# Layer-norm statistics from rows instead of from partition blocks, in an attention kernel that is bound by TensorE

## The chip, the cores and the metric

One core of one Trainium2 chip. The metric is the device time of one execution in microseconds (us).

## The reference

128 graphs of 128 nodes with 768 features. Cut to what matters:

```python
h = jnp.maximum(_layernorm(x, axis=-1), 0.0)          # mean and variance over 768, eps 1e-5
q, k, v = (split_heads(h @ W + b) for W, b in ...)    # 12 heads of 64
scores = q @ k.T / sqrt(64) + beta * adj              # -9e15 where adj == 0
out = x + softmax(scores) @ v
```

All is float32.

## The kernel before

The 128 graphs go in 32 groups of 4. In each group TensorE computes three "slices" of projections, called qk0, v and qk1, with a scheme of 15 block products a slice in place of 18. The scores and the weighted sums of the attention stand between these products. While TensorE works on group G, the other engines prepare group G + 1. `then(n, f)` hangs work behind product n of a slice; the scheduler may place it earlier in an engine's queue, unless `tc.issue_after(ins)` queues it behind the instruction `ins` of the same engine (order alone, no wait).

x is loaded in blocks: partition block a of 32 holds features 192a to 192a + 191, so that VectorE's transpose of 32 x 32 squares later gives the layout TensorE needs. A row's 768 features then lie in four partition blocks, and its statistics must be summed over partitions. Two small matmuls do that:

```python
def stats(G, g):                       # VectorE: 16 of these a group
    ...
    for b in range(NB):
        nc.vector.bn_stats(st[G][:, g * NB + b, :], xg[G, g][:, b, :])

def moments_1(G, lo, hi):
    bank = pm[G, lo, "bank"] = take()
    ...
    for q in range(0, P, HD):          # sums over the four blocks
        nc.tensor.matmul(pm[G, lo][q:q + HD, 0], mean8...[:, q:q + HD], halves(G, lo, hi, 1), start=True, stop=True)
    nc.vector.tensor_reduce(mean, ...)
    ...                                # three more small VectorE instructions
def moments_2(G, lo, hi, mean, d):
    for q in range(0, P, HD):
        nc.tensor.matmul(pm[G, lo][q:q + HD, 1], mean8...[:, q:q + HD], d, start=True, stop=True)
    ...
    nc.gpsimd.tensor_tensor(r, ve, nhalf.to_broadcast([P, n]), ALU.pow)      # 128 x 16
    shifted = nc.gpsimd.tensor_tensor(t, mean, r, ALU.mult)

def norm(G, g):                        # ScalarE: 16 a group
    for b in range(NB):
        ...
        nc.scalar.activation(t, t, AF.Relu, bias=shift[G, n], scale=rstd[G, n])
```

The adjacency of the next group passes through VectorE, and its square through ScalarE:

```python
def bias_1(G, raw):
    nc.vector.transpose(a, raw...)                                   # adjT
    nc.vector.tensor_scalar(kp, a, 0.0, None, op0=ALU.is_gt)
    nc.vector.tensor_scalar(a, a, beta_c, ..., op0=ALU.mult, op1=ALU.min)
    ...                                                              # GpSimd fills t
    nc.vector.copy_predicated(t, kp, a)                              # biasT
    if G:
        nc.scalar.activation(a, a, AF.Square, scale=...)             # square
def bias_2(G, a):
    nc.vector.tensor_reduce(bm, a, AX.X, ALU.max)                    # the maximum, reads the square
    nc.vector.tensor_tensor(seen[:, 16:20], seen[:, 16:20], bm, ALU.max)
```

The partial sums of the products lie in PSUM banks, 8 in all. After its product, VectorE adds a bank to its result (L352, L361) or ScalarE copies it (L357). TensorE may write a bank again only after that.

## Time and profile before

| | before |
|---|---|
| time, median of 6 runs | 2892.97 us (2892.39 to 2894.02) |
| span of the profiled run | 2891.4 us |
| busy: TensorE, VectorE, ScalarE, GpSimd | 100%, 68%, 28%, 13% |
| one steady group | 89.40 us |

The prediction below shows the lines of this profile. The way to read it: TensorE is busy in every window from its beginning to its end, at full clock. What does not take TensorE's time, and does not let it wait, costs nothing.

### The profile page before, as it was taken

The numbers are of one execution on the slowest core, as the hardware profiler recorded it, in microseconds if no ns is written. First come the engines' busy times: TensorE is split into PE (matmuls) and PEld (weight loads), VectorE is DVE, ScalarE is ACT, GpSimd is POOL, SyncE is SP. The second block draws the span as 40 slices with busy tenths as digits, with TensorE's granted clock in tenths as the row PEclk, the third lists the DMA queues.
The fourth block names the chain that finished last, engine by engine and source line by source line (L and its number), as shares of the span: only waits on it lengthen the run. The fifth ranks groups of instructions, "written<-read, shape, count | busy, mean of one in ns | idle before, by whom it ended". The sixth has DMA issues, their size and how long they took to land.

```text
span 2891.4 us, 81358 instructions
## 1 busy us (share of the span) xinstructions
PE 2879.8 (100%) x35562; PEld 2020.5 (70%) x35562; DVE 1961.4 (68%) x4743; ACT 801.3 (28%) x1750; POOL 370.9 (13%) x304
## 2 busy tenths in 40 slices
PE   9999999999999999999999999999999999999999
PEld 7666677666777676777667766677666677666766
DVE  7866667666676666767667676667666676666665
ACT  2432322222222323223232232322223222322221
POOL 1111111111111111111111111111111111111110
PEclk9999999999999999999999999999999999999999
DMA  6322122221222111221112212122221222111211
GB/s 166 78 56 57 39 62 71 60 56 44 54 71 63 52 51 47 71 68 52 56 42 67 71 50 61 40 63 71 56 60 39 58 71 60 56 48 47 67 41 39
DMA packets 357784, 172.16 MB, mean 60 GB/s; under 512 B 84400, under 2 KB 357040, under 8 KB 357424
## 3 DMA queue, kind: packets, MB, share of 16 engines
q1 hardware_dynamic: 355552, 166.53, 21.3%
q8 instruction: 279, 4.57, 0.7%
q10 hardware_dynamic: 1872, 0.40, 0.1%
q14 instruction: 81, 0.66, 0.1%
HBM read 116.53 MB, written 50.33 MB: 58 GB/s over the span
## 4 chain that ended last, share of the span: by engine, by line
PE 96%; issue 2%; DVE 1%; DMA 0%; POOL 0%; ACT 0%; SPq 0%; ACTq 0%; POOLq 0%; DVEq 0%
PE bank L336 82%; PE bank L382 6%; PE bank L417 6%; PE bank L498 1%; DMA x<-in_x_dram 0%; POOL rstd L262 0%; DVE S L286 0%; ACT x L273 0%; DVE qk L361 0%; POOL xo L422 0%; PE bank L241 0%; DVE A L280 0%; PE bank L255 0%; PE bank L437 0%; PE bank L549 0%
## 5 line engine op out<-in xcount | busy, mean ns | idle before, releaser
L336 PE MATMUL bank<-S,qk_T 128*64 128x256 f32 x7056 | 822.6, 380 | 1.1 <-ACT qk L357 0.8
L336 PEld LDWEIGHTS bank<-S,qk_T 128*64 128x64 f32 x7056 | 503.4, 137 | 257.6 <-issue 4.1
L361 DVE TENSOR_TENSOR qk<-qk,bank 128x512 f32<-128x512 f32 x630 | 428.6, 681 | 340.1 <-PE bank L336 338.1
L357 ACT ACTIVATE qk<-bank,bqk 128x256 f32<-128x256 f32 x756 | 311.5, 471 | 1010.6 <-PE bank L336 812.6
L336 PE MATMUL bank<-A,qk_T 128*64 128x256 f32 x4032 | 478.6, 379 | 0.9 <-DVE qk L361 0.9
L336 PE MATMUL bank<-S,qk_B 128*64 128x256 f32 x4032 | 478.2, 379 | 1.0 <-DVE qk L361 1.0
L422 POOL TENSOR_TENSOR xo<-xo,o 128x512 f32<-128x512 f32 x189 | 252.2, 1334 | 1601.4 <-DVE o L401 1343.3
L336 PE MATMUL bank<-v_T,S 128*64 128x256 f32 x3584 | 422.6, 380 | 0.0
L352 DVE TENSOR_TENSOR v<-v,bank 128x512 f32<-128x512 f32 x320 | 220.0, 687 | 296.1 <-PE bank L336 296.1
L389 ACT ACTIVATE e<-e 128x512 f32<-128x512 f32 x378 | 227.2, 630 | 661.0 <-DVE e L386 660.5
L336 PEld LDWEIGHTS bank<-A,qk_T 128*64 128x64 f32 x4032 | 284.3, 137 | 137.5 <-DVE qk L361 1.1
L336 PEld LDWEIGHTS bank<-S,qk_B 128*64 128x64 f32 x4032 | 278.6, 137 | 128.9 <-DVE qk L361 1.5
L336 PEld LDWEIGHTS bank<-v_T,S 128*64 128x64 f32 x3584 | 252.3, 137 | 126.3 <-issue 5.7
L273 ACT ACTIVATE x<-x,shift,rstd 128x192 f32<-128x192 f32 x504 | 224.3, 533 | 350.1 <-POOL shift L264 350.1
L336 PE MATMUL bank<-v_B,S 128*64 128x256 f32 x2048 | 244.1, 380 | 0.0
L386 DVE SCALAR_TENSOR_TENSOR e<-bank,biasT 128x512 f32<-128x512 f32 x378 | 231.2, 680 | 16.7 <-PE bank L382 16.7
L336 PE MATMUL bank<-v_T,A 128*64 128x256 f32 x2048 | 237.9, 379 | 0.0
L417 PEld LDWEIGHTS bank<-v,e 128*64 128x64 f32 x6048 | 208.6, 138 | 27.3
L280 DVE STREAM_TRANSPOSE A<-x 128x256 f32<-128x256 f32 x378 | 212.0, 613 | 4.0 <-ACT x L273 4.0
L417 PE MATMUL bank<-v,e 128*64 128x65 f32 x6048 | 208.3, 221 | 0.0
L347 DVE TENSOR_TENSOR v<-bv_b,bank 128x512 f32<-128x512 f32 x192 | 131.8, 686 | 112.0 <-PE bank L336 112.0
L230 DVE BATCH_NORM_STATS2 st<-x 128x6 f32<-128x192 f32 x504 | 154.3, 344 | 76.5 <-DMA x<-in_x_dram 76.4
(83 smaller groups left out, 1688.3 us busy)
## 6 DMA issues: line engine op xcount, KB each, us to landing
x<-in_x_dram SPq DMA_DIRECT2D x504, 96.0 KB, 2.6
xo<-in_x_dram SPq DMA_DIRECT2D x189, 256.0 KB, 2.9
out_dram<-xo SPq DMA_DIRECT2D x189, 256.0 KB, 2.5
adj<-in_adj_dram SPq DMA_DIRECT2D x128, 64.0 KB, 2.4
qk_T<-in_L_gnn_Wq_dram SPq DMA_DIRECT2D x10, 128.0 KB, 4.1
qk_T<-in_L_gnn_Wk_dram SPq DMA_DIRECT2D x10, 128.0 KB, 4.0
v_T<-in_L_gnn_Wv_dram SPq DMA_DIRECT2D x5, 256.0 KB, 6.0
qk_B<-in_L_gnn_Wq_dram SPq DMA_DIRECT2D x8, 128.0 KB, 3.9
```

The lines of the kernel that those rows point to most:

```text
L230: nc.vector.bn_stats(st[G][:, g * NB + b, :], xg[G, g][:, b, :])
L273: nc.scalar.activation(t, t, AF.Relu, bias=shift[G, n], scale=rstd[G, n])
L280: last = nc.vector.transpose(t[:, :, g * N:(g + 1) * N].rearrange("p c (b i) -> p c b i", i=SQ), src)
L336: nc.tensor.matmul(p[q:q + HD, i, :], lhs[:, q:q + HD], rhs, start=(first and i == 0 and c == 0), stop=(c == 1), skip_group_check=True)
L352: added[G] = nc.vector.tensor_tensor(o, o, got, ALU.add if sign > 0 else ALU.subtract)
L357: nc.scalar.activation(t[:, i, :], p[:, i, :], AF.Identity, bias=bqk[:, i, oc:oc + 1], scale=float(sign))
L361: added[G] = nc.vector.tensor_tensor(t, t, p, ALU.add if sign > 0 else ALU.subtract)
L382: nc.tensor.matmul(ps[oc, i][k:k + HD, g * N:(g + 1) * N], t[r, 1, at][:, k:k + HD], t[r, 0, at], start=True, stop=True)
L386: taken[0] = nc.vector.scalar_tensor_tensor(e, ps[oc, i].rearrange("p (g n) -> p g n", g=GRP), SCORE_CAP * ISCALE, biasT[G], op0=ALU.min, ...
L389: nc.scalar.activation(e, e, AF.Exp, scale=1.0 / ISCALE)
L417: nc.tensor.matmul(pa[q:q + HD, 2 * g + i, :], es[G, oc, i][:, 2 * r + g, q:q + HD], vt[G, "v", r, h // 4][:, 4 * g + h % 4, :], start=Tru ...
L422: nc.gpsimd.tensor_add(t, t, o.rearrange("p a (b j) d -> p (a b) (j d)", j=2))
```

## The change

Its intent is to take the two sums over partitions off TensorE. x is loaded a second time, by rows, so that VectorE can compute a row's statistics alone. The results are then a column per row and must be spread to the four partition blocks; 16 transfers of 1 KB from SBUF to SBUF do that. SBUF is full, so the half rows use the two adjacency buffers. The adjacency is therefore loaded after them (and ahead of the small transfers), and its VectorE work is queued in v instead of floating into qk0. Cut to its core:

```diff
+    def load_halves(G, g):
+        for h in range(2):
+            t = rows[G, g, h] = work.tile([P, VH], F32, tag=("adj", "adjT")[h], ..., bufs=1)
+            nc.sync.dma_start(t, x[G * GRP + g, :, h * VH:(h + 1) * VH])
+    def row_stats(G, g):
+        ...
+        for h in range(2):
+            nc.vector.bn_stats(rows[G][:, g, h, :], rows[G, g, h])
+        nc.vector.bn_aggr(rows[G, "mv"][:, g, :], rows[G][:, g])
+    def row_moments(G):
+        ...
+        nc.gpsimd.tensor_tensor(t[:, 0], ve, nhalf.to_broadcast([P, GRP]), ALU.pow)      # 128 x 4
+        nc.gpsimd.tensor_tensor(t[:, 1], mean, t[:, 0], ALU.mult)
+        for b in range(NB):
+            for a in range(NB):
+                nc.sync.dma_start(to[a * SQ:(a + 1) * SQ, b], t[b * SQ:(b + 1) * SQ])
+        def behind(f, *args):
+            with tc.issue_after(added[G].ins):      # added: the latest add of a product
+                return f(*args)
 ... in qk0 of group G
-                    then(11 + g, lambda g=g: stats(G + 1, g))
+                    then((0, 5, 8, 11)[g], lambda g=g: load_halves(G + 1, g))
+                    then((4, 7, 10, 13)[g], lambda g=g: behind(row_stats, G + 1, g))
+            if G > 1:
+                then(14, lambda: raw.append(load_adj(G + 1)))
+                then(14, lambda: row_moments(G + 1))
 ... in v of group G
-                then(at + 5 + g, lambda g=g: norm(G + 1, g))
+                then(at + 5 + g, lambda g=g: behind(norm, G + 1, g) if G > 1 else norm(G + 1, g))
-            then(at, lambda: got.extend(moments_1(G + 1, 0, GRP * NB)))
-            then(at + (3 if G else 2), lambda: moments_2(G + 1, 0, GRP * NB, *got[:2]))
+            if G < 2:
+                ... (the two lines above)
-                then(8, lambda: got.append(bias_1(G + 1, load_adj(G + 1))))
+                then(8, lambda: got.append(behind(bias_1, G + 1, raw.pop()) if raw else bias_1(G + 1, load_adj(G + 1))))
```

The `behind` around the normalization orders nothing: `added` is an instruction of VectorE, the normalization runs on ScalarE, and `issue_after` orders within one engine only.

More of the change, by code (lines that the diff above doesn't have):

```diff
@@ L267, in moments_2 @@
         return shifted
+    rows = {}
+    def load_halves(G, g):
+        for h in range(2):
+            t = rows[G, g, h] = work.tile([P, VH], F32, tag=("adj", "adjT")[h], name=f"half_{G}_{g}_{h}", bufs=1)
+            nc.sync.dma_start(t, x[G * GRP + g, :, h * VH:(h + 1) * VH])
+    def row_stats(G, g):
+        if g == 0:
+            rows[G] = stat.tile([P, GRP, 2, nc.vector.BN_STATS_DIM], F32, tag="strow", name=f"strow_{G}", bufs=1)
+            rows[G, "mv"] = stat.tile([P, GRP, nc.vector.BN_AGGR_DIM], F32, tag="mvrow", name=f"mvrow_{G}", bufs=1)
+        for h in range(2):
+            nc.vector.bn_stats(rows[G][:, g, h, :], rows[G, g, h])
+        nc.vector.bn_aggr(rows[G, "mv"][:, g, :], rows[G][:, g])
+    def row_moments(G):
+        mv = rows[G, "mv"]
+        ve = stat.tile([P, GRP], F32, tag="verow", name=f"verow_{G}", bufs=1)
+        nc.vector.tensor_scalar(ve, mv[:, :, 1], EPS, None, op0=ALU.add)
+        mean = stat.tile([P, GRP], F32, tag="meanrow", name=f"meanrow_{G}", bufs=1)
+        nc.vector.tensor_scalar(mean, mv[:, :, 0], -1.0, None, op0=ALU.mult)
+        t = stat.tile([P, 2, GRP], F32, tag="row2", name=f"row2_{G}", bufs=1)
+        nc.gpsimd.tensor_tensor(t[:, 0], ve, nhalf.to_broadcast([P, GRP]), ALU.pow)
+        nc.gpsimd.tensor_tensor(t[:, 1], mean, t[:, 0], ALU.mult)
+        to = stat.tile([P, NB, 2, GRP], F32, tag="block2", name=f"block2_{G}", bufs=1)
+        for b in range(NB):
+            for a in range(NB):
+                nc.sync.dma_start(to[a * SQ:(a + 1) * SQ, b], t[b * SQ:(b + 1) * SQ])
+        for g in range(GRP):
+            for b in range(NB):
+                rstd[G, g * NB + b], shift[G, g * NB + b] = to[:, b, 0, g:g + 1], to[:, b, 1, g:g + 1]
     def norm(G, g):
@@ L524, in rows_1 @@
         t = xg[0, g].rearrange("p b f -> p (b f)")
-        s = stat.tile([P, 2, nc.vector.BN_STATS_DIM], F32, tag="strow", name=f"strow_{g}", bufs=2)
+        s = stat.tile([P, 2, nc.vector.BN_STATS_DIM], F32, tag="strow_0", name=f"strow0_{g}", bufs=2)
         for h in range(2):
@@ L530, in rows_1 @@
                 nc.vector.bn_stats(s[:, h, :], t[:, h * VH:(h + 1) * VH])
-        mv = stat.tile([P, nc.vector.BN_AGGR_DIM], F32, tag="mvrow", name=f"mvrow_{g}", bufs=2)
+        mv = stat.tile([P, nc.vector.BN_AGGR_DIM], F32, tag="mvrow_0", name=f"mvrow0_{g}", bufs=2)
         nc.vector.bn_aggr(mv, s)
-        ve = stat.tile([P, 1], F32, tag="verow", name=f"verow_{g}", bufs=2)
+        ve = stat.tile([P, 1], F32, tag="verow_0", name=f"verow0_{g}", bufs=2)
         first["ve"] = nc.vector.tensor_scalar(ve, mv[:, 1:2], EPS, None, op0=ALU.add)
@@ L609, in behind_scores @@
             return f(*args)
-    early = []
+    early, raw = [], []
     for G in range(NG):
@@ L626, in direct @@
                 elif G:
-                    then(11 + g, lambda g=g: stats(G + 1, g))
+                    then((0, 5, 8, 11)[g], lambda g=g: load_halves(G + 1, g))
+                    then((4, 7, 10, 13)[g], lambda g=g: behind(row_stats, G + 1, g))
+            if G > 1:
+                raw = []
+                then(14, lambda: raw.append(load_adj(G + 1)))
+                then(14, lambda: row_moments(G + 1))
         if not G:
@@ L650, in direct @@
                     then(g, lambda g=g: stats(G + 1, g))
-                then(at + 5 + g, lambda g=g: norm(G + 1, g))
-            then(at, lambda: got.extend(moments_1(G + 1, 0, GRP * NB)))
-            then(at + (3 if G else 2), lambda: moments_2(G + 1, 0, GRP * NB, *got[:2]))
+                then(at + 5 + g, lambda g=g: behind(norm, G + 1, g) if G > 1 else norm(G + 1, g))
+            if G < 2:
+                then(at, lambda: got.extend(moments_1(G + 1, 0, GRP * NB)))
+                then(at + (3 if G else 2), lambda: moments_2(G + 1, 0, GRP * NB, *got[:2]))
             if G:
-                then(8, lambda: got.append(bias_1(G + 1, load_adj(G + 1))))
-                then(12, lambda: bias_2(G + 1, got[2]))
+                then(8, lambda: got.append(behind(bias_1, G + 1, raw.pop()) if raw else bias_1(G + 1, load_adj(G + 1))))
+                then(12, lambda: bias_2(G + 1, got[-1]))
             else:
```

## The prediction

> **What bounds the kernel now.** I read first the page's busy shares and its chain of what ended last, then the windows of one steady group of four graphs (31.6 us of first projection slice "qk0", 29.1 of "v", 28.7 of "qk1"), then the timelines of TensorE, VectorE, ScalarE and the DMA queue over that group. The page:
>
> ```profile
> span 2891.4 us, 81358 instructions
> PE 2879.8 (100%) x35562; PEld 2020.5 (70%) x35562; DVE 1961.4 (68%) x4743; ACT 801.3 (28%) x1750; POOL 370.9 (13%) x304
> ...
> PE 96%; issue 2%; DVE 1%; DMA 0%; POOL 0%; ACT 0%; SPq 0%; ACTq 0%; POOLq 0%; DVEq 0%
> ```
>
> TensorE is busy for all but 11.6 us, and the chain runs through it for 96%. A busy PE need not be at its peak, so I looked at the distance between starts. The windows are qk1, qk0 and v of one group:
>
> ```profile
> 1507.18:1535.88 28.70, 28.70 (x338) 20.06 (x336) 23.46 (x63) 5.03 (x12) 4.19 (x3) 1.00 0.29 82
> 1535.88:1567.52 31.64, 31.64 (x434) 22.58 (x432) 21.67 (x57) 8.99 (x19) 4.34 (x4) 1.00 0.29 78
> 1567.52:1596.59 29.07, 29.07 (x347) 19.91 (x345) 15.52 (x28) 10.73 (x22) 3.13 (x2) 1.00 0.04 11
> ```
>
> In every window the first figure, the length, equals the second, PE busy; the clock is 1.00. VectorE has 5.2, 10.0 and 13.6 us idle in them. The group takes 89.40 us, and so does the next. Each block product (16 matmul records) starts 1.72 to 1.73 us after the one before. So only work taken off TensorE's own stream, or a new wait of TensorE, moves the time. The PE timeline where the change cuts:
>
> ```profile
> 1573.86 3.67 PE L336 MATMUL bank<-v_T,S 128*64 128x256 f32 x32
> 1577.36 0.26 PE L241 MATMUL bank<-st,mean 128*64 128x32 f32 x4
> 1577.45 1.93 PE L336 MATMUL bank<-v_B,S 128*64 128x256 f32 x16
> 1579.20 1.90 PE L336 MATMUL bank<-v_T,S 128*64 128x256 f32 x16
> 1580.93 1.90 PE L336 MATMUL bank<-v_B,S 128*64 128x256 f32 x16
> 1582.66 0.26 PE L255 MATMUL bank<-dev,mean 128*64 128x32 f32 x4
> 1582.74 1.93 PE L336 MATMUL bank<-v_T,S 128*64 128x256 f32 x16
> 1584.50 1.90 PE L336 MATMUL bank<-v_T,A 128*64 128x256 f32 x16
> ```
>
> The matmuls of L241 and L255 sum the layer norm's statistics over the four partition blocks. They stand in the stream with no wait before them.
>
> **What the Trainium skill says.** (1) "TensorE: Matmul & The Clock Gate", section "Back-to-back issue gap": a matmul of 1 to 64 columns still takes about 60 cycles, a floor of some 25 ns, and one of 256 columns 262 cycles. The trace agrees nearly: 1.725 us over 16 records is 108 ns, and the small ones come out at 29 ns below. (2) "Perfetto Trace Analysis", section "Per-instruction lifecycle": the end of a TensorE record is estimated from its size, so I use starts and not the 0.26 us; and VectorE and ScalarE are strict first-in-first-out, so that one instruction waiting for a transfer holds up all behind it. The trace of before shows such waits (76.4 us, below). (3) "DMA: Bandwidth & Descriptors", section "Anatomy of one DMA": about 2.0 us of fixed cost per transfer, most of it completion; the page of before has medians of 2.4 to 2.9 us from issue to landing. (4) The same page, "Specifications": under 512 B a transfer is off line rate. The new results go in pieces of 32 B; before's trace has none so small, and 1 KB per transfer leaves only the fixed part.
>
> **The change, part by part.** It applies from the third group on: 29 of the 32 groups get their statistics this way (the order of the built program confirms it: exactly 29 pairs of L241 and of L255 are gone from PE, nothing else there changes).
>
> *Removed from TensorE.* From the starts: L241 to its next product 0.09 us, and that product's distance to the next is 1.75 instead of 1.725, so 0.115. L255: 0.08, and 1.76 instead of 1.725, so 0.115. Together 0.23 us a group for 8 records, 29 ns each. 29 groups x 0.23 = **6.7 us**, all on the path.
>
> *VectorE*, off the path. Removed a group: 16 BN_STATS of 192 columns (344 ns: 5.5 us) and six small ones of 174 to 198 ns (1.1 us). Added: 8 BN_STATS of 384 columns (the first group's rows have 552 ns: 4.4), 4 aggregates (209 ns: 0.8), two small scalings (0.15 each: 0.3). 6.6 less 5.5 is 1.1 us a group less, 31 us in all, worth nothing by itself with 28.8 us idle a group.
>
> *GpSimd*: the power on 128x16 takes 2905 ns, on 128x8 1673, so some 1.05 us on 128x4 by the same slope; off the path.
>
> *DMA*: 8 loads of 192 KB more a group, 29 x 1.57 MB = 46 MB on 116.5 MB read. DMA share rises from 21% to perhaps 27%. The queue of issues gets 8 + 16 more entries a group at about 0.4 us each (below: 2.70 us for 6, 0.38 for one), 10 us of 89.
>
> *Moved*: the adjacency's VectorE work (transpose, compare, scale, select, maximum: 0.70 + 0.43 + 0.48 + 0.77 + 0.69, with a small one 3.2 us) goes from qk0, where the scheduler had put it beside the scores, to products 8 to 10 of v, where VectorE waits about 1 us in every 1.73. It delays one or two adds by about 0.6 to 0.8 us. A partial-sum bank is used again two to four products later (3.45 us or more), and adds take 0.69, so up to about 2.5 us of delay is free.
>
> **Does the new chain come in time?** Lines of before that I date it by:
>
> ```profile
> DVE st L230 <- DMA x<-in_x_dram: 76.4, 71, 2.5
> ...
> 1587.26 7.12 ACT L273 ACTIVATE x<-x,shift,rstd 128x192 f32<-128x192 f32 x16 [10.64 <-POOL shift L264]
> ...
> 1597.41 3.28 DVE L280 STREAM_TRANSPOSE A<-x 128x256 f32<-128x256 f32 x6
> ...
> 1555.35 0.38 SPq L369 DMA_DIRECT2D xo<-in_x_dram  x1
> 1605.09 2.70 SPq L155 DMA_DIRECT2D x<-in_x_dram  x6
> ```
>
> In before, normalization starts at 1587.26 because GpSimd's result is late, and ends at 1594.4; its reader begins at 1597.41. After: the last row statistics stand behind product 13 of qk0 (about 1566.5 to 1567.8), the two scalings behind the last product (1568.9), the power to 1570.3; the adjacency's four loads are issued ahead (to about 1571); 16 issues x 0.4 = 6.4 us to 1577.5, plus 2 to 2.5 to landing: **1580**. ScalarE needs the first block's four results only to start, near 1575.5, and has 16 x 0.45 and two left-over exponentials: done near 1586, some 11 us ahead of the transposes. The adjacency's square then follows its select at about 1589.6, so VectorE's maximum does not wait long for it.
>
> The half loads: one buffer per half, so each load waits for the statistics before it. Half 1 can be issued at about 1548.8 and is read at 1554.3; half 2, queued behind a store and its reload (about 1555.7), at 1556.1 and is read at 1560.4; half 3 at 1562.2, read at 1566.5. That leaves 4.2 to 5.5 us for 384 KB (and a 256 KB reload ahead), against 2.9 us for 256 KB on the page. So VectorE may wait some tenths of a us; TensorE should not.
>
> Sum: 2893.45 - 6.7 = **2886.8 us**, -0.23%.
>
> **Rivals.** *(a) A transfer on the path.* A half load late by more than about 2.5 us stops VectorE's queue, and with it the bank TensorE wants. For: four waits a group on single buffers, in a queue with 24 more entries. Against: the 71 waits of up to 2.5 us in before cost TensorE nothing. At 1 us of loss a group it would be 29 us: 2916 (+0.8%). *(b) The small transfers late*, if 32 B pieces cost far more than estimated: over 11 us of delay makes transposes late and then the next group's sums. Each us beyond is 29 us; three would be 2973, slower by over 2%. Its room is large, so I hold it under 3%. *(c) Nothing gained*, the small matmuls hiding in gaps that stay: about 2893. Against: starts around them shift by the full 0.115. *(d) A gain of over 2%* would need 2 us a group off TensorE; nothing there but 0.23 goes.
>
> **Range and chances.** The three runs of before span 1.1 us and the working is good to about 1 us, so 2885 to 2888 if nothing else happens (about 80%). Small waits at some places may give back a part, seldom all: range 2884.5 to 2891.5. Faster by over 2%: 0.01; within 2%: 0.97; slower: 0.02.
>
> **What would show it.** Right: no L241/L255 in v from the third group on; a group's period 89.17; PE busy equal to the window's length; the normalization begun near 1575 to 1577 of the same group; VectorE waiting for half loads, TensorE not. Wrong: idle TensorE before L336 products or score matmuls named to VectorE's adds; normalization ending after the transposes' place; product starts over 1.73 us apart in the second half of qk0.

## The result, and the profile after

| | before | after |
|---|---|---|
| time, median of 6 runs | 2892.97 us | 2884.99 us (2884.47 to 2885.43) |
| span of the profiled run | 2891.4 us | 2882.7 us |
| one steady group | 89.40 us | 89.17 us |
| VectorE busy in one group | 60.65 us | 60.39 us |
| DMA: share of 16 engines, HBM read | about 22%, 117 MB | about 28%, 162 MB |

The ratio is 0.9972 (95% interval 0.9959 to 0.9985). Ratios are the mean time of one kernel's fast runs over that of the other's of the same rounds, so they are not quite the ratio of the medians quoted. The gain of the medians is 7.98 us; 6.7 us was predicted.

The changed kernel's page, its busy shares and chain (line numbers are 35 higher than before: L371 is the product, formerly L336):

```profile
PE 2872.4 (100%) x35330; PEld 2014.5 (70%) x35330; DVE 1955.9 (68%) x4511; ACT 806.5 (28%) x1750; POOL 316.9 (11%) x304
...
PE 99%; DVE 1%; issue 0%; POOL 0%; POOLq 0%
```

TensorE has 232 records fewer (35562 less 35330), exactly 29 x 8, and is still the whole chain. The windows of qk1, qk0 and v of one group, to be read like those of before in the prediction (length, then busy time of TensorE, its weight loads, VectorE, ScalarE and GpSimd, then TensorE's clock, the DMA share and GB/s):

```profile
1413.14:1441.84 28.70, 28.70 (x338) 19.94 (x336) 22.95 (x56) 5.03 (x12) 4.21 (x3) 1.00 0.30 85
1441.84:1473.47 31.63, 31.63 (x434) 22.34 (x432) 19.70 (x52) 8.54 (x18) 4.33 (x4) 1.00 0.35 104
1473.47:1502.30 28.83, 28.83 (x338) 19.72 (x336) 17.75 (x32) 11.32 (x23) 1.22 (x2) 1.00 0.16 34
```

TensorE is still busy for the whole length; v is shorter by 0.24 us than before, the other two by 0.01 at most. The PE timeline at the place where L241 and L255 were:

```profile
1479.81 3.67 PE L371 MATMUL bank<-v_T,S 128*64 128x256 f32 x32
1483.31 1.90 PE L371 MATMUL bank<-v_B,S 128*64 128x256 f32 x16
1485.04 1.90 PE L371 MATMUL bank<-v_T,S 128*64 128x256 f32 x16
1486.76 1.90 PE L371 MATMUL bank<-v_B,S 128*64 128x256 f32 x16
```

The products now follow each other at 1.72 to 1.73 us without a break.

**Where the 8 us come from.** I followed both timelines by one mark, the start of the score matmuls, of which each group has one block in qk0 and one in v. From v to the next qk0 a steady group of before takes 57.77 us and one of after 57.53 to 57.54, in all 29 groups: 29 x 0.235 = 6.8 us. In before, four groups take longer: 58.14, 58.17, 58.02 and 57.93, which is 0.37 + 0.40 + 0.25 + 0.16 = 1.2 us more. After has none of these. The sum is **8.0 us**, the gain of the medians. (The runs of one kernel spread by 1.0 to 1.6 us, so that an agreement to 0.1 us is partly luck.) One of the four places, in the timelines of VectorE and then of TensorE and its weight loads, before:

```profile
544.38 0.36 DVE L230 BATCH_NORM_STATS2 st<-x 128x6 f32<-128x192 f32 x1 [2.36 <-DMA x<-in_x_dram]
549.56 0.68 DVE L361 TENSOR_TENSOR qk<-qk,bank 128x512 f32<-128x512 f32 x1
550.29 3.22 PEld L336 LDWEIGHTS bank<-S,qk_T 128*64 128x64 f32 x32 [0.61 <-DVE qk L361]
```

The bracket gives the idle time before an instruction and what ended it. The scheduler had put the old statistics early, in qk1, between transposes and sums. VectorE waits 2.36 us for a load, then works without a pause until 550, so that it stays late; the add at 549.56 is late, and TensorE waits for its bank. The other three places have waits of VectorE of 2.40, 2.24 and 2.16 us.

The two profiled spans differ by 8.7 us, not 8.0. Some 0.55 us of the rest is chance, in the first group: an add of GpSimd and a two-input instruction of VectorE start within 0.1 us of each other, and one of them has to wait for the other. Before (VectorE waits), then after (GpSimd waits):

```profile
89.94 1.29 POOL L422 TENSOR_TENSOR xo<-xo,o 128x512 f32<-128x512 f32 x1 [20.85 <-ACT o L404]
90.01 1.76 DVE L203 SCALAR_TENSOR_TENSOR qk_T<-qk_T,qk_B 128x512 f32<-128x512 f32 x1
```

```profile
89.92 2.50 POOL L457 TENSOR_TENSOR xo<-xo,o 128x512 f32<-128x512 f32 x1 [20.88 <-ACT o L439]
90.00 0.69 DVE L203 SCALAR_TENSOR_TENSOR qk_T<-qk_T,qk_B 128x512 f32<-128x512 f32 x1
```

That it is chance is seen in two experiments below that differ only after this point: in small_matmuls_back VectorE waits (1.76 us), in small_matmuls_twice GpSimd does (2.49 us).

**The new chain.** Timelines of the issuing queue, ScalarE and VectorE after, in the group whose v begins at 1473.47:

```profile
1474.13 2.05 SPq L329 DMA_DIRECT2D adj<-in_adj_dram  x4
1476.23 10.56 SPq L299 DMA_DIRECT2D block<-row  x16
...
1481.28 0.53 ACT L308 ACTIVATE x<-x,block 128x192 f32<-128x192 f32 x1
1488.88 1.86 ACT L308 ACTIVATE x<-x,block 128x192 f32<-128x192 f32 x4 [1.10 <-DMA block<-row]
1495.74 0.63 ACT L346 ACTIVATE adjT<-adjT 128x512 f32<-128x512 f32 x1 [5.00 <-DVE biasT L340]
...
1496.40 0.69 DVE L350 TENSOR_REDUCE bm<-adjT 128x4 f32<-128x512 f32 x1
```

The transfers take 0.66 us each of the queue, not 0.4. The normalization (L308) still ends at 1490.74, long before the transposes at 1503.13 that read it. What stands behind it on ScalarE, the adjacency's square, has its 5.00 us idle for VectorE's select, not for the normalization. All half loads together let VectorE wait 1.7 us in five places, and TensorE nowhere.

### The profile page after: what moved, and what is told of

Same layout as the page of the kernel before. It is cut to its first block, busy times and chain, and to the rows that moved or that the text cites.

```text
span 2882.7 us, 81559 instructions
## 1 busy us (share of the span) xinstructions
PE 2872.4 (100%) x35330; PEld 2014.5 (70%) x35330; DVE 1955.9 (68%) x4511; ACT 806.5 (28%) x1750; POOL 316.9 (11%) x304
## 4 chain that ended last, share of the span: by engine, by line
PE 99%; DVE 1%; issue 0%; POOL 0%; POOLq 0%
PE bank L371 85%; PE bank L417 6%; PE bank L452 6%; PE bank L533 1%; PE bank L595 0%; DVE A L315 0%; DVE qk_T L206 0%; DVE qk L396 0%; DVE S L321 0%; DVE e L421 0%; PE bank L472 0%; PE bank L489 0%; PE bank L584 0%; DVE e L476 0%; DVE xo L497 0%
## 5 line engine op out<-in xcount | busy, mean ns | idle before, releaser
L371 PE MATMUL bank<-S,qk_T 128*64 128x256 f32 x7056 | 822.5, 379 | 0.8 <-ACT qk L392 0.8
L371 PEld LDWEIGHTS bank<-S,qk_T 128*64 128x64 f32 x7056 | 503.8, 137 | 256.1 <-ACT e L424 5.2
L371 PE MATMUL bank<-S,qk_B 128*64 128x256 f32 x4032 | 478.2, 379 | 1.0 <-DVE qk L396 1.0
L371 PE MATMUL bank<-A,qk_T 128*64 128x256 f32 x4032 | 478.6, 379 | 0.4 <-DVE qk L396 0.4
L371 PE MATMUL bank<-v_T,S 128*64 128x256 f32 x3584 | 421.8, 380 | 0.0
L371 PEld LDWEIGHTS bank<-A,qk_T 128*64 128x64 f32 x4032 | 284.3, 137 | 137.0 <-DVE qk L396 0.5
L371 PEld LDWEIGHTS bank<-S,qk_B 128*64 128x64 f32 x4032 | 278.6, 137 | 128.9 <-DVE qk L396 1.4
L371 PEld LDWEIGHTS bank<-v_T,S 128*64 128x64 f32 x3584 | 254.7, 137 | 130.4 <-issue 5.7
L421 DVE SCALAR_TENSOR_TENSOR e<-bank,biasT 128x512 f32<-128x512 f32 x378 | 231.7, 682 | 109.1 <-PE bank L417 109.1
L371 PE MATMUL bank<-v_B,S 128*64 128x256 f32 x2048 | 243.2, 379 | 0.0
L371 PE MATMUL bank<-v_T,A 128*64 128x256 f32 x2048 | 237.9, 379 | 0.0
L308 ACT ACTIVATE x<-x,block 128x192 f32<-128x192 f32 x464 | 217.3, 535 | 39.9 <-DMA block<-row 39.1
L371 PEld LDWEIGHTS bank<-v_B,S 128*64 128x64 f32 x2048 | 147.1, 137 | 73.9
```

What stands on the lines that cost most here:

```text
L371: nc.tensor.matmul(p[q:q + HD, i, :], lhs[:, q:q + HD], rhs, start=(first and i == 0 and c == 0), stop=(c == 1), skip_group_check=True)
L421: taken[0] = nc.vector.scalar_tensor_tensor(e, ps[oc, i].rearrange("p (g n) -> p g n", g=GRP), SCORE_CAP * ISCALE, biasT[G], op0=ALU.min, ...
```

## The experiments

Theory A: the gain is TensorE's time for 232 small records (29 ns each, 6.8 us), plus four waits of before (1.2 us). Rival B: the small matmuls hide, and the gain comes from a freer VectorE or queue. Theory C: VectorE's and ScalarE's order costs nothing until a wait at the head of VectorE's queue is longer than the room of the banks, some 2.5 us; beyond that TensorE loses the excess. Its rivals differ by run. All kernels gave the right result. Each group of runs below (1 to 4; 5, 6, 8 and 9; 7 and 10) was sent to one chip, with its own runs of before there.

### 1 and 2. The small matmuls put back, once and twice

```diff
+            def small(m):                      # behind products 3 and 6 of v, 29 groups
+                ...
+                for _ in range(1):             # run 2: range(2)
+                    for q in range(0, P, HD):
+                        nc.tensor.matmul(kept[0][q:q + HD, m * SQ:(m + 1) * SQ], mean8...[:, q:q + HD], ident[:, 0:SQ], start=True, stop=True)
```

The edit is on the changed kernel; nobody reads the bank.

> The changed kernel with the removed TensorE work put back as dead work: in 29 groups 4 matmuls (8 records) of 64 weight columns by 32 columns behind products 3 and 6 of v, on a constant, into a bank nobody reads. Theory A (the gain is the TensorE time of these matmuls, 29 ns a record, plus some 1.2 us of waits of TensorE for late VectorE adds in four places of before): 29 x 0.235 = 6.8 us slower than the changed kernel, 2891.8, a group's period 89.40 again, and no waits named to VectorE in those four places. Rival B (the gain comes from VectorE and the queue, the matmuls hide): no slower than the changed kernel, 2885.

> The same with twice as many (16 records a group). Theory A: another 6.8 us, 2898.6, period 89.63 to 89.64: the cost is linear in the records. Rival: a fixed cost for breaking the stream of 256-column products (a change of form), then less than 1 us more than with the single set.

Measured: 2891.84 us with one set (before on that chip 2892.76; ratio 0.9996) and 2898.39 with two (ratio 1.0018). The steps are 6.85 from the changed kernel's 2884.99 and 6.55 between the two. A group's v-to-qk0 stretch is 57.77 and then 58.00 us. TensorE's timeline of small_matmuls_twice:

```profile
1489.58 0.38 PE L715 MATMUL bank<-ident,mean 128*64 128x32 f32 x8
1489.79 1.93 PE L371 MATMUL bank<-v_B,S 128*64 128x256 f32 x16
1491.54 1.90 PE L371 MATMUL bank<-v_T,S 128*64 128x256 f32 x16
```

Eight records, from 1489.58 to 1489.79, take 0.21 us, and the next product 0.02 to 0.03 more: twice the 0.115 of four. So the cost is per record, and B falls: VectorE, the queue and the row statistics are those of the changed kernel here, and the gain is gone, but for the four waits (neither run has them).

### 3. The old statistics pinned

```diff
-                    then(11 + g, lambda g=g: stats(G + 1, g))
+                    then(11 + g, lambda g=g: behind(stats, G + 1, g))     # issue_after(added[G])
```

The edit is on the kernel before.

> The kernel before, with nothing but its statistics on VectorE queued behind the add of their product in qk0, where before the scheduler had put them early, beside the arriving loads. Theory A: the four waits of TensorE for a late add (0.40 to 0.64 us, each some 6 us behind a wait of VectorE for a load of 2.16 to 2.40 us) vanish, period 89.40 throughout, 1.2 us faster than before, near 2891.8. Rival: these waits have another cause; then they stay and the time is that of before.

Measured: 2891.64 us, against 2892.76 of before (medians; 1.1 us; ratio 0.9994 with an interval that holds 1, so that the time alone would not prove it). The trace does: every group now takes 57.76 to 57.77 us, the four long ones are gone, and VectorE's waits for x loads fall from 76.4 us to 1.7. The line of VectorE's waits in this run (total, times, longest), whose like for before stands in the prediction:

```profile
DVE st L230 <- DMA x<-in_x_dram: 1.7, 2, 1.0
```

The fixed place is thus worth 1.2 us by itself, with the old statistics as well.

### 4 and 5. The adjacency's part alone

On the kernel before: the adjacency loaded behind product 14 of qk0, its VectorE work queued behind product 8 of v. Run 5 also moves the maximum:

```diff
+            if G > 1:
+                raw = []
+                then(14, lambda: raw.append(load_adj(G + 1)))
-                then(8, lambda: got.append(bias_1(G + 1, load_adj(G + 1))))
+                then(8, lambda: got.append(behind(bias_1, G + 1, raw.pop()) if raw else bias_1(G + 1, load_adj(G + 1))))
 run 5 only:
-                then(12, lambda: bias_2(G + 1, got[-1]))
+                then(14 if G > 1 else 12, lambda: behind(bias_2, G + 1, got[-1]) if G > 1 else bias_2(G + 1, got[-1]))
```

> The kernel before with the adjacency's part of the change alone: its load at the end of qk0, its VectorE work queued behind product 8 of v. Theory A: it takes nothing off TensorE, so the time is that of before within 1 us; the four waits may stay or move. Rival: clearing 3.2 us of VectorE work out of qk0 gives part of the gain, 2 us or more.

Measured: **2916.10 us**, 23 us slower than before (ratio 1.0079, 1.0065 to 1.0092). Neither theory had that. ScalarE's, VectorE's and TensorE's timelines of this run, in one group:

```profile
1419.07 6.24 ACT L273 ACTIVATE x<-x,shift,rstd 128x192 f32<-128x192 f32 x14 [10.64 <-POOL shift L264]
1425.22 0.61 ACT L311 ACTIVATE adjT<-adjT 128x512 f32<-128x512 f32 x1
1425.87 0.69 DVE L315 TENSOR_REDUCE bm<-adjT 128x4 f32<-128x512 f32 x1 [3.46 <-ACT adjT L311]
1427.40 1.95 PE L336 MATMUL bank<-v_T,S 128*64 128x256 f32 x16 [0.56 <-DVE v L352]
```

The old normalization begins late (at 1419.07, when GpSimd is done). The square, now in v too, stands behind 14 of its instructions; VectorE's maximum waits 3.46 us for the square; two adds wait behind the maximum; TensorE waits for a bank. The group takes 58.55 us from v to qk0 in place of 57.77: 0.78 lost for a wait of 3.46.

> The run adjacency_alone took 23 us more than before. Its trace: VectorE's maximum over the adjacency waits 3.46 us a group for its square on ScalarE, which stands behind 14 normalizations (these begin late, at GpSimd's result), and behind the maximum wait two adds, of which TensorE waits for one (0.56 to 0.8 us in each of 29 groups). This kernel is the same with the maximum alone moved behind the last product of v. Theory C (that wait is the whole loss): VectorE's wait and TensorE's 29 waits vanish, 2892 to 2893.5, as before. Rival: the adjacency's 2.4 us of VectorE work between the adds is itself the loss; then the time stays near 2916.

Measured: 2892.99 us against 2893.01 of before (ratio 1.0). The wait for the square was the whole loss, and moving 2.4 us of VectorE work into v costs nothing. With the maximum where the change has it, both parts therefore belong together: the adjacency's new place is then free only because the row statistics let the normalization end early.

### 6 and 7. Where the adjacency stands

On the changed kernel. Run 6 drops the fixed place of the adjacency's VectorE work, run 7 puts its load behind the small transfers.

```diff
 run 6:
-                ... behind(bias_1, G + 1, raw.pop()) if raw else ...
+                ... bias_1(G + 1, raw.pop()) if raw else ...
 run 7:
-                then(14, lambda: raw.append(load_adj(G + 1)))
                 then(14, lambda: row_moments(G + 1))
+                then(14, lambda: raw.append(load_adj(G + 1)))
```

> The changed kernel without the fixed place of the adjacency's VectorE work (its load stays ahead of the small transfers): the scheduler puts it among the six score evictions of v. Theory C (VectorE's order matters only where a wait at its head is longer than about 2 us, the room of the banks): the maximum then waits for a square that stands behind some normalizations and so behind the small transfers, about 1 to 2 us; TensorE loses little, 2885 to 2900. Rival: the fixed place is worth much by itself, over 2915.

> The changed kernel with the adjacency's load behind the small transfers in the queue (the scheduler puts one of its four ahead, three behind). The transfers take 10.56 us, so the last adjacency parts are issued some 1.5 us later than the last transfer and land near 1.5 us before to 0.5 us after VectorE's transpose of the adjacency. Theory C: a wait of VectorE of at most 1 us, under the room of 2.67: 2885, no loss. Rival (the load ahead is what makes the change work): slower by 0.5 us a group or more, over 2899.

Measured: 2885.26 us (ratio 0.9973) and 2885.10 us (ratio 0.9974), both as the changed kernel. In run 6 the maximum waits 19.5 us in 29 groups (at most 1.7), under the room. So neither the load ahead nor the fixed place of the adjacency is worth anything measurable when it alone is taken away.

### 8. Nothing at a fixed place

```diff
-                    then((4, 7, 10, 13)[g], lambda g=g: behind(row_stats, G + 1, g))
+                    then((4, 7, 10, 13)[g], lambda g=g: row_stats(G + 1, g))
-                ... behind(bias_1, G + 1, raw.pop()) if raw else ...
+                ... bias_1(G + 1, raw.pop()) if raw else ...
```

> The changed kernel with neither row statistics nor adjacency at fixed places (no queueing behind an add). The scheduler then puts parts of the row statistics among score evictions, sends the small transfers between stores, and puts the normalizations ahead of evictions of the next slice on ScalarE. Theory C: new waits at the heads of VectorE's and ScalarE's queues, some longer than the banks allow: slower than the changed kernel by 0.3 to 3 us a group, 2894 to 2970. Rival: the places do not matter, 2885.

Measured: **3097.59 us** (ratio 1.0713), worse than expected. Run 6 differs from this one by the row statistics' place alone, so that place is worth 212 us. VectorE's and TensorE's timelines, and the longest of TensorE's waits (total, times, longest):

```profile
1500.72 0.56 DVE L283 BATCH_NORM_STATS2 strow<-half 128x6 f32<-128x384 f32 x1 [7.17 <-DMA half<-in_x_dram]
1501.92 3.68 PE L371 MATMUL bank<-v_T,S 128*64 128x256 f32 x16 [4.45 <-DVE e L421]
...
PE bank L371 <- DVE e L421: 133.2, 27, 6.0
```

The scheduler has put row statistics ahead of the score evictions (L421), where they wait 7.17 us for a half row. The scores hold six of the eight banks, so TensorE stops. The last line says that TensorE waits 133.2 us in 27 such places. It doesn't only wait: the product after the stop takes 3.68 us in place of 1.90, at a lower clock (see run 9). The mean granted clock of this profile is 0.978, that of the changed kernel's 0.999. By that, up to 0.021 x 3095 = 65 us of the 212 are the clock's, an estimate.

### 9. The small transfers doubled

```diff
-                nc.sync.dma_start(to[a * SQ:(a + 1) * SQ, b], t[b * SQ:(b + 1) * SQ])
+                for s in range(0, SQ, SQ // 2):
+                    nc.sync.dma_start(to[a * SQ + s:a * SQ + s + SQ // 2, b], t[b * SQ + s:b * SQ + s + SQ // 2])
```

> The changed kernel with each small transfer in two of 16 partitions, 32 a group. In the changed kernel 16 take 10.56 us of the issuing queue (0.66 us each). Theory C: if an issue stays at 0.66, they end 10.6 us later; the normalization then ends near the place of the transposes, but before that the adjacency's square stands behind it on ScalarE and VectorE's maximum waits some 5 us for it, which costs TensorE 2 to 3 us a group: 2945 to 2970. If an issue of half the pieces takes 0.4 us, the end moves by only 2 us and nothing is lost. Rival (my prediction's 11 us of room up to the transposes): 2885 in either case.

Measured: **3010.43 us** (ratio 1.0396), 125 us over the changed kernel, more than expected. The queue, VectorE and TensorE in one group, and TensorE in three others:

```profile
1544.29 22.23 SPq L300 DMA_DIRECT2D block<-row  x32
1570.12 0.69 DVE L351 TENSOR_REDUCE bm<-adjT 128x4 f32<-128x512 f32 x1 [5.75 <-ACT adjT L347]
1571.65 1.95 PE L372 MATMUL bank<-v_T,S 128*64 128x256 f32 x16 [2.84 <-DVE v L388]
...
1009.37 3.68 PE L372 MATMUL bank<-v_T,S 128*64 128x256 f32 x16 [4.01 <-DVE v L388]
539.80 3.60 PE L372 MATMUL bank<-v_T,S 128*64 128x256 f32 x16 [2.10 <-DVE v L388]
1756.60 1.95 PE L372 MATMUL bank<-v_T,S 128*64 128x256 f32 x16 [3.35 <-DVE v L388]
```

Half the pieces cost the queue as much: 22.23 / 32 = 0.69 us each. In this group the normalization ends 28.0 us after v's start, 10.7 us later than in the changed kernel, the square stands behind it, and the maximum waits 5.75 us. The group of 1571.65 takes 60.60 us in place of 57.53: 3.07 lost. 5.75 - 3.07 = 2.68, and in run 4 it was 3.46 - 0.78 = 2.68: the room of the banks at this place is 2.7 us, and beyond it TensorE loses the excess one for one. In all 11 groups of this run in which the clock stays full the difference is 2.68 or 2.69, for waits of 4.88 to 6.26 us. The other 18 groups lose more than this rule says, 4 to 7.7 us, because TensorE's clock drops: at 1009.37, after 4.01 us idle, a product takes 3.68 us in place of 1.90, and the granted clock of the stretch from 1009.4 to 1016.0 is 0.64. "TensorE: Matmul & The Clock Gate", section "The HAM clock gate", of the Trainium skill describes this state: the clock is halved after an idle window. My expectation had left it out. The maximum's waits of all 29 groups add up to 174.6 us; less 29 times the room, that is 97 of the 134 us by which this profile is longer than the changed kernel's. The rest, some 37 us, I put down to the clock (an estimate; no run separates the two).

### 10. One buffer for both half rows

```diff
-            t = rows[G, g, h] = work.tile([P, VH], F32, tag=("adj", "adjT")[h], name=f"half_{G}_{g}_{h}", bufs=1)
+            t = rows[G, g, h] = work.tile([P, VH], F32, tag="adj", name=f"half_{G}_{g}_{h}", bufs=1)
```

> The changed kernel with one buffer for both half rows, so that each second half is loaded only after the statistics of the first: VectorE waits for a load four times more a group, some 2.5 to 3.5 us each (a half load lands 2.8 us after its issue), in qk0. The two runs before give TensorE's loss as VectorE's wait less about 2.67 us (3.46 gives 0.80; 5.75 gives 3.08), for one wait in v. Theory C: in qk0 the waits follow every 6 us with the attention's work on VectorE between, so that lateness adds up: 1 to 3 us lost a group, 2915 to 2975. Rival (each wait is below or near the room, nothing is lost): 2885 to 2890.

Measured: 2941.83 us (ratio 1.0179; 4 runs), 57 us or 2 us a group over the changed kernel, within the expectation, but not quite by its mechanism. VectorE waits 274.7 us for half rows in 174 places. TensorE waits for VectorE mostly in one place a group:

```profile
1420.08 0.56 DVE L283 BATCH_NORM_STATS2 strow<-half 128x6 f32<-128x384 f32 x1 [3.59 <-DMA half<-in_x_dram]
1422.40 2.73 PE L371 MATMUL bank<-v_T,S 128*64 128x256 f32 x16 [2.68 <-DVE e L421]
```

The last half's statistics come to stand ahead of the score evictions of v, as in run 8. The place shown is one of the worst: the clock dropped there too (2.73 us in place of 1.90), as at two other such stops; over the whole profile it is 0.997. The waits inside qk0, nearer to 1 us, pass mostly without loss.

A version with own buffers for the half rows, which would have left the adjacency where it was, didn't build: the pool wanted 99.5 KB a partition, and 99.19 were left. No experiment beat the changed kernel.

## Why the prediction was right

- **The bound, and that only TensorE's stream counts**: right. A group takes 89.17 us, the figure the prediction named, and all 29 are alike. ("From the third group on" should read: from group index 3, the fourth.)
- **0.23 us a group, 6.7 us**: right, 0.235 and 6.8. Runs 1 and 2 show that it is the cost of the records themselves.
- **The rest of the sum was short by 1.2 us.** The failed step is in rival (a): "the 71 waits of up to 2.5 us in before cost TensorE nothing". In four places of 71 they did, 0.16 to 0.41 us each. I had read them from TensorE's busy windows in one steady group, which has none; the waits of TensorE's weight loads over the whole span name VectorE's add seven times, 4.8 us in all, and these four places are among them. Run 3 shows the cause. (The sum also started from 2893.45 us, the median of three runs; that of six is 2892.97.)
- **VectorE**: the durations were right (a BN_STATS of 384 columns 549 ns, an aggregate 209), the difference not: 5.5 us less busy in all, not 31. Part of the reason is that durations of neighbours overlap, which a sum of durations leaves out: four old statistics back to back take 1.14 us together, not 4 x 344 ns. The rest of the difference isn't traced. Off the path, this was worth nothing, as said.
- **GpSimd** takes 1.02 us for the power, and 1.05 was estimated. **The issues** of the small transfers cost 0.66 us each, not 0.4; the last was issued some 3 us later than predicted (1486.8, which is 13.3 us after v's start, against 10.0), but ScalarE was done 17.3 us after v's start, where 18.5 had been predicted, since it needs only four results at a time. That the trace of before has no pieces as small as 32 B was a misreading: its loads of the two biases and of beta, at the start, go in pieces of 4 B by the kernel's text. Nothing rests on it.
- **"Some 11 us ahead of the transposes"** was right as a distance (12.4), but wrong as the room it was used for in rival (b). The transposes are not the first that suffer: the square and VectorE's maximum are. Run 9 made the chain some 11.7 us longer in the queue and lost 125 us, where (b), which charged only what goes beyond 11 us, would have had some 20 at most. The true room is about 5 us until the square is delayed, and 2.7 us more until TensorE is.
- **"Up to about 2.5 us of delay is free"**: right in v, 2.68 us by two runs. In qk1, where VectorE has no pause to catch up, a wait of 2.16 us already cost 0.16, while one of 2.53 us ahead of the score evictions of qk0 cost nothing. So it is the place that decides, not the length alone.
- **The half loads** were judged rightly: VectorE waits 1.7 us for them in all.

## What to carry to other kernels

Where one engine is busy without a gap, the worth of a change is the time between starts that it removes there, and it can be read to 0.01 us from the timeline before the change is made; but look over the whole span for the few places where the bound engine waits. A long chain off the path is as safe as its tightest reader, and that can be a small instruction behind it in some engine's queue, not the one the data is meant for. In queues that a scheduler orders, put work that waits for a transfer at a place of your choosing: here that alone decided between 2885 and 3098 us.

## What the Trainium skill lacked or had wrong

- "DMA: Bandwidth & Descriptors", section "Issuing engines are not separate DMA queues", calls the time to issue a transfer usually small relative to the transfer itself. Its breakdown in the section "Anatomy of one DMA", with some 50 ns of dispatch, is for transfers that GpSimd issues; these are issued by SyncE. Here the 1 KB transfers from SBUF to SBUF took 0.66 us each of the queue (16 in 10.56 us), and those of 0.5 KB 0.69 (32 in 22.23 us), by number and not by size, while a transfer landed in 1.7 us. For a row of small transfers the issue is the larger cost. The nearest figures are a few hundred ns of setup on the page "SBUF — State Buffer" (section "The DMA setup-cost knee") and a count of cycles in this page's part on trn3, for earlier generations. No page has a measured issue time for trn2.
- "TensorE: Matmul & The Clock Gate", section "The HAM clock gate": the clock is said to drop after an idle window of about 3.4 us. In run 9 the product after a wait of 2.10 us took 3.60 us, nearly twice its 1.90, so the drop is seen after shorter waits than that. After a wait of 3.35 us at another place it took 1.95, which the page's figure allows. In that run all waits over 3.4 us were followed by a slow product, and some of those from 2.10 to 3.4.
- The same page, section "Back-to-back issue gap": the floor for up to 64 columns is given as about 25 ns; a record of 32 columns with its weight load cost 29 ns here (0.115 us for four), inside a stream of 256-column products. Near, but it is the figure to use for such pairs.
- "SBUF — State Buffer", section "Who interferes with whom", says that a two-input instruction of VectorE and a GpSimd instruction that reads SBUF block each other whole, the one that issues first winning. The runs agree that one waits for the other (VectorE 1.76 in place of 0.69 us, or GpSimd 2.50 in place of 1.29); but in both profiles GpSimd has the earlier start, by 0.07 and 0.08 us, so that the winner can't be told from the starts that a profile shows.
- No page of the skill tells how to find out how long VectorE may wait before TensorE lacks a PSUM bank: here 2.7 us at one place, from the waits and losses of two runs.
